# A graph layer on one core: VectorE's share of column copies 86.4 loads an octet in place of 85.33, and the end of the run in another order

## Chip, core and metric

The kernel runs on one core of one Trainium2 chip. The metric is the device time of one execution in microseconds, the median of several runs. Before the change it is 3294.95 us (three runs, 3292.81 to 3297.97).

## What is computed

A message passing step over 12500 nodes of 64 features and 400000 edges, sorted by destination, followed by a residual and a layer norm:

```python
m_in = jnp.concatenate([x[src], x[dst], edge_attr], axis=-1)    # 64 + 64 + 16
h = jax.nn.silu(m_in @ W1 + b1)
messages = jax.nn.silu(h @ W2 + b2)
agg = jax.ops.segment_sum(messages, dst, num_segments=12500)
node = jax.nn.silu(jnp.concatenate([x, agg], axis=-1) @ W3 + b3)
out = layernorm(x + node)
```

## The kernel before

The 400000 edges are 3125 tiles of 128, and eight tiles are an **octet** (391 of them; the last has five). The main loop (line 759) runs over octets. Since edges are sorted by destination, the targets of an octet lie within a window of 48 nodes, and sums of a window are made by a product with a one-hot matrix.

What an octet needs is the features of its edges' sources, tile by tile, and the kernel has three ways to get them, so that several engines share the work:

- **Gathers.** GpSimd issues one indirect DMA for each tile (`gather`, line 448), three octets ahead; five buffers `ga`.
- **Column copies.** Two tiles (a pair) can instead be filled column by column from node features that lie in SBUF (`columns`, lines 336 to 370), by ScalarE (line 367) or VectorE (line 369). The addresses are loaded into the engine's registers first, up to 16 (ScalarE) or 32 (VectorE) at a time; a column takes two of them, as the pair's two tiles lie on the two halves of the partitions. A full pair of 128 columns takes 256 loads.
- **Row copies.** SyncE fills a pair by 256 DMAs of one row (`rows`, line 397).

`shares` (line 314) tells how many loads each engine makes in an octet, in up to four parts of it. ScalarE makes 80 in four octets of five and 64 in the fifth. VectorE makes 96 in two octets of three and 64 in the third, as three or two chunks of 32. Lines 327 to 332 turn that into pairs: as soon as an engine has made 256 more loads, a pair of the octet after next is taken from the gathers. They go up to octet `len(octs) - QUIET - 2`, exclusive.

Through one turn `o` of the main loop, in the order that is written out by hand for TensorE, ScalarE, VectorE and SyncE: TensorE turns the one-hot matrix of octet o+1 (line 515) and computes its window's part (472); VectorE adds a finished window sum to `agg` (`add_window`, 592, six octets behind, three in the last eight), compares targets for o+2 (497), and makes its first chunk of columns; TensorE puts the sources in place and adds the edges' part (550, 553, 554) and ScalarE applies the first silu (557); VectorE copies window and one-hot matrix (477, 525) and makes its other chunks; TensorE makes window sums of an earlier octet (`add_up`, 581) and the second layer of another (566, 568), with ScalarE's second silu (572). The window sums lie in four slots of one PSUM tile, and TensorE's `add_up` waits for the last fold (592) ahead of it.

The nodes are finished in 25 groups of up to 512: `node_begin`, `node_x`, `node_sums` (619, 624, 630), `node_silu` (636), `node_add`, `node_stats`, then the root, the division (660) and `store` (664). All but the last two groups are spread over the main loop. The last two come at its end: the last but one in turn NO - 1 (lines 819 to 828; NO is 391), with the limits (701 to 718), which check that the windows held; the last behind the loop (881 to 893). The last group has 212 nodes, 53 partitions. `verdict` (720) sums the limits into `badi`, a flag; behind it all, every engine loads that flag into a register (line 106) and branches over a general version (line 108) that isn't run with these inputs.

Of the kernel before, what the change touches and what calls it, by code (L numbers as in the profile page):

```python
# [20 lines left out]
P = 128  # L21
G = 4
# [10 lines left out]
BEGIN = 6  # L33
TABLES = 7
ACOLS = (48, 32)
VCOLS = (32, 0, 32, 32)
ROWS = (256, 15)
LOADS = (16, 32)
XADDR = 16640
X2ADDR = XADDR + 50528  # L40
# [1 line left out]
HALF = 6144  # L42
OVER = 304
TURN = 195
QUIET = 5
DRAIN = 8
LAG = CT * P // 32
AHEADS = 256
# [6 lines left out]
@with_exitstack  # L55
def kernel(
    ctx: ExitStack,
    tc: tile.TileContext,
    x: bass.AP,
    xt: bass.AP,  # L60
    xt2: bass.AP,
    src_c: bass.AP,
    src_row: bass.AP,
    src_pair: bass.AP,
    dst_c: bass.AP,
    dst_row: bass.AP,
    attr_t: bass.AP,
    attr_2: bass.AP,
    base: bass.AP,
    w1: bass.AP,  # L70
    b1: bass.AP,
    w2: bass.AP,
    b2: bass.AP,
    w3: bass.AP,
    b3: bass.AP,
    out: bass.AP,
    edges: int,
):

    nc = tc.nc
    N, D = x.shape

    const = ctx.enter_context(tc.tile_pool(name="const", bufs=1))
    dram = ctx.enter_context(tc.tile_pool(name="dram", bufs=1, space=DRAM))
    pa = dram.tile([N, D], F32, name="pa")
    badi = const.tile([1, 1], I32, name="badi")
    ident = const.tile([P, P], F32, name="ident")
    make_identity(nc, ident)
    identb = const.tile([P, P], BF16, name="identb")  # L100
    nc.vector.tensor_copy(identb, ident)

    with ExitStack() as inner:
        windows(inner, tc, ident, identb, badi, pa, x, xt, xt2, src_c, src_row, src_pair, dst_c, dst_row, attr_t, attr_2, base, w1, b1, w2, b2, w3, b3, out, edges)

    flag = nc.values_load(badi[0:1, 0:1], min_val=0, max_val=4 * P,
                          skip_runtime_bounds_check_because="a count of partitions")
    with tc.If(flag > 0):
        general(tc, ident, x, xt, src_c, dst_c, dst_row, attr_t, w1, b1, w2, b2, w3, b3, out, edges)


def windows(ctx, tc, ident, identb, badi, pa, x, xt, xt2, src_c, src_row, src_pair, dst_c, dst_row, attr_t, attr_2, base, w1, b1, w2, b2, w3, b3, out, edges):
    nc = tc.nc
# [4 lines left out]
    NO = base.shape[1]  # L118
# [176 lines left out]
    with tc.tile_pool(name="gat", bufs=AHEAD + 2) as gat, \  # L295
# [18 lines left out]
        def shares(eng, o):  # L314
            if o < BEGIN:
                return (0, 0, 0, 0)
            if eng == ENG.Activation:
                return ACOLS if (o - BEGIN) % 5 < 4 else (ACOLS[0] - 16, ACOLS[1])
            return VCOLS if (o - BEGIN) % 3 < 2 else VCOLS[:3] + (0,)

        counts = {}
        for eng in (ENG.Activation, ENG.DVE):
# [274 lines left out]
        NG = len(groups)  # L597
        RB = 5
        v = nv.tile([P, 2 * RB, G, D], F32, name="v")
# [56 lines left out]
        def divide(q, i):  # L656
            p = groups[q][1] // G
            vi = v[:p, q % (2 * RB), i, :]
            j = q * G + i
            nc.vector.tensor_scalar(vi, vi, mv[:p, j, 0:1], rstd[:p, j:j + 1], op0=OP.subtract, op1=OP.mult)  # L660

        def store(q):
            c, n = groups[q]
            nc.sync.dma_start(out[c:c + n, :].rearrange("(p i) d -> p i d", i=G), v[:n // G, q % (2 * RB)])

# [11 lines left out]
        for q in range(rest):  # L679
            o = lead[due[q]] + LAST - 1  # L680
# [10 lines left out]
        for q0, q1 in batches:  # L691
            o = lead[due[q1 - 1]] + LAST + 2 * G
# [27 lines left out]
        def verdict(bad):  # L720
            pc = mis.tile([1, 4], F32, name="mm")
            nc.tensor.matmul(pc, onec, bad, start=True, stop=True)
            bs = nv.tile([1, 1], F32, name="bs")
            nc.vector.tensor_reduce(bs, pc, AX.X, OP.add)
            nc.vector.tensor_copy(badi, bs)
# [10 lines left out]
        folds = times({None: LAST, **{k: 3 for k in range(DRAIN)}})  # L736
# [17 lines left out]
        with tc.manual_schedule(engines={ENG.PE, ENG.Activation, ENG.DVE, ENG.SP}):  # L754
# [4 lines left out]
            for o in range(NO + 2):  # L759
# [3 lines left out]
                for k in range(0, NA, XC)[3 * o - 3:3 * o] if o else []:  # L763
                    n = min(XC, NA - k)
# [33 lines left out]
                for b in range(0, NO, 4):  # L798
                    if o == b + (4 if b < NO - DRAIN else 2):
                        bases(ENG.DVE, b)  # L800
                for q in folds.get(o, []):
                    add_window(q)
                if o == 1:
                    relative(0, CT, SCT)
                for k in range(3 * o - 3, 3 * o) if 1 <= o < 6 else []:
                    if k < 2 * len(parts):
                        c = parts[k // 2]
# [5 lines left out]
                def behind():  # L813
                    for q in adds.get(o, []):
                        add_up(q)
                    for q in seconds.get(o, []):
                        second_layer(q)

                if o == NO - 1:
                    assert NG == rest + 2 and groups[rest][0] + groups[rest][1] + LAG <= (NO - 4) // (CT // OT) * STEP  # L820
                    behind()
                    for i in range(G):
                        node_sums(rest, i)
                    node_silu(rest)
                    node_add(rest)
                    for i in range(G):
                        node_stats(rest, i)
                    bad = limits()
# [48 lines left out]
            for i in range(NO + 2, NO + LAST):  # L877
                for q in folds.get(i, []):
                    add_window(q)
            assert NO not in todo  # L880
            for i in range(G):
                node_sums(rest + 1, i)
            node_silu(rest + 1)
            node_add(rest + 1)
            for i in range(G):
                node_stats(rest + 1, i)
            verdict(bad)
            root(rest, NG)
            inverse(rest, NG)
            for q in range(rest, NG):  # L890
                for i in range(G):
                    divide(q, i)
                store(q)


@with_exitstack
# [255 lines left out]
```

## Time and profile before

| | before |
|---|---|
| median of three runs | 3294.95 us |
| the profiled execution | 3292.35 us |
| its span, first to last instruction | 3290.6 us |
| busy: ScalarE | 3109.2 us, 94% |
| busy: TensorE | 2486.1 us, 76% |
| busy: GpSimd | 2465.6 us, 75% |
| busy: VectorE | 2042.4 us, 62% |
| mean granted TensorE clock | 0.71 |
| column copies on ScalarE and VectorE | 14464 and 16000 |
| row copies | 6400 |

The profile comes from one execution. PE is TensorE, PEld its weight loads, DVE VectorE, ACT ScalarE, POOL GpSimd, SP SyncE; a q behind the name is its sequencer or its DMA queue. Loading registers, branches, semaphores and issuing DMAs don't count as busy. "issue" is idle time of an engine in which it waited for nothing that the profile shows; register loads fall into it. Window rows give the stretch, its length, the engine's busy time and its count of instructions, then the granted clock, the busy share of the DMA engines and GB/s.

### The profile page before, as it was taken

How to read it: one execution, taken by the hardware profiler on the slowest of the kernel's cores; microseconds unless marked ns; L12 is line 12 of the kernel's file. 1: busy time of each engine (PE TensorE's matmuls, PEld its weight loads, DVE VectorE, ACT ScalarE, POOL GpSimd, SP SyncE). 2: the span in 40 equal slices, each digit the busy share in tenths (PEclk: the TensorE clock that was granted, in tenths of full speed). 3: DMA queues.
4: the chain of work that ended last, by engine and by line, in shares of the span. 5: the costliest groups of instructions: out<-in, count | busy, mean ns of one | idle time of the engine just before them, and what ended most of it. 6: DMA issues, size and time to landing. Idle time of an engine off the chain costs nothing. (4 is left out here: it accounts for less than half of the span.)

```text
span 3290.6 us, 88339 instructions
## 1 busy us (share of the span) xinstructions
PE 2486.1 (76%) x15344; PEld 1705.0 (52%) x15344; DVE 2042.4 (62%) x18296; ACT 3109.2 (94%) x15306; POOL 2465.6 (75%) x2607
## 2 busy tenths in 40 slices
PE   7867777777777777767777777777877867777786
PEld 5545555555555545544454554545545545554554
DVE  5566666666666666666666666666666666666652
ACT  2799999999999999999999999999999999999991
POOL 7777777777777777777777777777777777777774
PEclk8787777777667677677767767766666676667666
DMA  7222222222222222221221222222222222222221
GB/s 148 50 41 40 43 41 40 43 41 40 45 44 44 42 42 40 41 43 38 48 46 39 43 41 40 43 43 43 45 41 42 40 44 41 43 44 45 39 42 33
DMA packets 160868, 147.82 MB, mean 45 GB/s; under 512 B 103748, under 2 KB 113718, under 8 KB 159526
## 3 DMA queue, kind: packets, MB, share of 16 engines
q0 software_dynamic: 83168, 85.33, 14.6%
q1 hardware_dynamic: 62624, 47.00, 5.7%
q10 hardware_dynamic: 14502, 9.75, 1.4%
q14 instruction: 447, 3.66, 0.4%
q8 instruction: 127, 2.08, 0.3%
HBM read 135.44 MB, written 6.40 MB: 43 GB/s over the span
## 5 line engine op out<-in xcount | busy, mean ns | idle before, releaser
L448 POOL DMA_INDIRECT ga<-pa,sc x2505 | 2375.6, 948 | 763.9 <-issue 666.0
L367 ACT ACTIVATE cx<-xs,x 128x1 f32 x14464 | 2789.5, 328 | 24.9 <-issue 19.5
L369 DVE TENSOR_TENSOR cx<-xs,x 128x4 uint8 x16000 | 1288.9, 154 | 1095.6 <-issue 1073.7
L581 PEld LDWEIGHTS pg<-eh,m 128*64 128x64 f32 x6250 | 296.8, 184 | 674.5 <-DVE agg L592 344.5
L550 PE MATMUL p<-ident,ga 128*128 128x128 f32 x1253 | 347.1, 364 | 393.7 <-DMA ga<-pa,sc 392.6
L568 PEld LDWEIGHTS p<-w2d,h 128*128 128x128 f32 x3126 | 536.7, 259 | 186.5 <-issue 186.5
L568 PE MATMUL p<-w2d,h 128*128 128x128 f32 x3126 | 632.5, 365 | 0.0
L554 PE MATMUL p<-oh,xw 128*128 128x512 f32 (+1 forms) x758 | 584.6, 866 | 0.0
L581 PE MATMUL pg<-eh,m 128*64 128x48 f32 x6250 | 352.8, 271 | 211.4 <-DVE agg L592 209.1
L550 PEld LDWEIGHTS p<-ident,ga 128*128 128x128 f32 x1253 | 220.4, 186 | 468.4 <-issue 433.2
L557 ACT ACTIVATE h<-p 128x512 f32<-128x512 f32 x391 | 243.1, 622 | 53.5 <-PE p L554 33.1
L515 PE MATMUL ph<-identb,eh 128*96 128x128 bf16 x1563 | 211.9, 276 | 99.9 <-DVE oh L525 96.4
L572 ACT ACTIVATE m<-p 128x512 f32<-128x512 f32 x391 | 242.6, 620 | 41.6 <-PE p L568 40.0
L525 DVE COPY oh<-ph 96x512 f32<-96x512 f32 x391 | 263.1, 673 | 1.9 <-PE ph L515 1.9
L515 PEld LDWEIGHTS <-eh 128*96 128x96 bf16 x1563 | 163.4, 163 | 136.5 <-DVE oh L525 122.4
L566 PE MATMUL p<-b2r,one 3*128 3x512 bf16 x391 | 193.3, 494 | 53.7 <-ACT m L572 53.2
L472 PE MATMUL mm<-w1bb,xr 65*96 65x128 f32 x782 | 221.5, 377 | 6.6 <-DMA xr<-in_xt 4.0
L497 DVE TENSOR_TENSOR eh<-wrow,dc 128x384 f32<-128x384 f32 x392 | 212.5, 542 | 11.3 <-PE wrow L624 6.9
L554 PEld LDWEIGHTS p<-oh,xw 128*128 128x128 f32 x758 | 175.8, 284 | 0.0
L472 PEld LDWEIGHTS mm<-w1bb,xr 65*96 65x96 f32 x782 | 139.9, 230 | 8.1 <-DMA xr<-in_xt 4.2
L553 PE MATMUL p<-cx,w1d 128*128 128x128 f32 x474 | 122.1, 368 | 0.0
L477 DVE TENSOR_TENSOR xw<-mm,mask 96x128 f32<-96x128 f32 x391 | 108.1, 276 | 20.6 <-PE mm L472 18.0
(106 smaller groups left out, 980.1 us busy)
## 6 DMA issues: line engine op xcount, KB each, us to landing
rx<-pa SPq DMA_DIRECT2D x6400, 0.2 KB
ga<-pa,sc POOLq DMA_INDIRECT x2505
oh<-in_attr SPq DMA_DIRECT2D x130, 192.0 KB
xr<-in_xt SPq DMA_DIRECT2D x391, 24.0 KB
cxi<-in_src_pair SPq DMA_DIRECT2D x238, 1.0 KB
xs<-in_xt ACTq DMA_DIRECT2D x6, 512.0 KB
pa<-v ACTq DMA_DIRECT2D x12, 256.0 KB
x<-in_xt ACTq DMA_DIRECT2D x6, 512.0 KB
```

The lines of the kernel that those rows point to most:

```text
L367: nc.scalar.activation(cols[key][:, k:k + 1], word(i, xb, XADDR), AF.Identity, bias=word(i + 4, x2b, X2ADDR))
L369: nc.vector.tensor_tensor(t[:, 4 * k:4 * k + 4], at(i, xb, XADDR), at(i + 4, x2b, X2ADDR), op=OP.max)
L448: nc.gpsimd.indirect_dma_start(out=ga[:, i, :], out_offset=None, in_=x if o < RAW else pa[:, :], in_offset=bass.IndirectOffsetOnAxis(ap=sc ...
L472: nc.tensor.matmul(pw[:E, :], winrow[o], w1bb.rearrange("k s m -> k (s m)"), start=True, stop=True)
L515: nc.tensor.matmul(ph[:E, i, :], eh[:, i, :, 1], identb, start=(i == 0), stop=(i == k - 1), skip_group_check=True)
L525: nc.vector.tensor_copy(oh[:E, :], ph[:E, :(n + 1) // 2].rearrange("p i e -> p (i e)"))
L550: nc.tensor.matmul(p1[:, i, :], g2.rearrange("p s d -> p (s d)"), ident, is_transpose=True, start=(i == c), stop=False, skip_group_check=True)
L554: nc.tensor.matmul(p1[:, :k], xw[o % 3], oh, start=False, stop=True, skip_group_check=True)
L557: nc.scalar.activation(h[:, :k], p1[:, :k], AF.Silu)
L568: nc.tensor.matmul(p2[:, 2 * i:2 * i + 2, :].rearrange("p s d -> p (s d)"), h[:, i, :], w2d, start=False, stop=(i == k - 1), skip_group_ch ...
L572: nc.scalar.activation(m[:, :n2], p2[:, :n2], AF.Silu)
L581: nc.tensor.matmul(pg[s * D:(s + 1) * D, :], m[:, i, :], eh[:, i // 2, :, s], start=(i < 2), stop=(i >= n - 2), skip_group_check=True)
```

## The change

VectorE's loads follow a rate of 27 chunks in 10 octets: an octet has three chunks or two, by the difference of a rounded line, 86.4 loads an octet. `QUIET` falls from 5 to 3. At the end, the fold that stood first in turn NO stands in turn NO - 1, behind that turn's sums and ahead of the node sums; the verdict stands ahead of the last group's sums; every engine loads the flag ahead of the last store; and `store` splits a group whose partitions are no multiple of 16, here 53 into 48 and 5.

```diff
+VRATE = (27, 10)
...
-QUIET = 5
+QUIET = 3
...
-        windows(inner, ...)
-
-    flag = nc.values_load(badi[0:1, 0:1], min_val=0, max_val=4 * P,
-                          skip_runtime_bounds_check_because="a count of partitions")
+        flag = windows(inner, ...)
+
     with tc.If(flag > 0):
...
-            return VCOLS if (o - BEGIN) % 3 < 2 else VCOLS[:3] + (0,)
+            n = (o + 1 - BEGIN) * VRATE[0] // VRATE[1] - (o - BEGIN) * VRATE[0] // VRATE[1]
+            return VCOLS if n == 3 else VCOLS[:3] + (0,)
...
         def store(q):
             c, n = groups[q]
-            nc.sync.dma_start(out[c:c + n, :].rearrange("(p i) d -> p i d", i=G), v[:n // G, q % (2 * RB)])
+            to, p = out[c:c + n, :].rearrange("(p i) d -> p i d", i=G), n // G
+            for a, b in ((0, p // 16 * 16), (p // 16 * 16, p)):
+                if b > a:
+                    nc.sync.dma_start(to[a:b], v[a:b, q % (2 * RB)])
...
-                for q in folds.get(o, []):
+                for q in folds.get(o, []) if o != NO else []:
                     add_window(q)
...
                 if o == NO - 1:
...
                     behind()
+                    for q in folds[NO]:
+                        add_window(q)
                     for i in range(G):
                         node_sums(rest, i)
...
             assert NO not in todo
+            verdict(bad)
             for i in range(G):
                 node_sums(rest + 1, i)
...
                 node_stats(rest + 1, i)
-            verdict(bad)
             root(rest, NG)
             inverse(rest, NG)
             for q in range(rest, NG):
                 for i in range(G):
                     divide(q, i)
+                if q == NG - 1:
+                    flag = nc.values_load(badi[0:1, 0:1], min_val=0, max_val=4 * P,
+                                          skip_runtime_bounds_check_because="a count of partitions")
                 store(q)
+    return flag
```

More of the change, by code (lines that the diff above doesn't have):

```diff
@@ L103 @@
     with ExitStack() as inner:
-        windows(inner, tc, ident, identb, badi, pa, x, xt, xt2, src_c, src_row, src_pair, dst_c, dst_row, attr_t, attr_2, base, w1, b1, w2, b2, w3, b3, out, edges)
-    flag = nc.values_load(badi[0:1, 0:1], min_val=0, max_val=4 * P,
-                          skip_runtime_bounds_check_because="a count of partitions")
+        flag = windows(inner, tc, ident, identb, badi, pa, x, xt, xt2, src_c, src_row, src_pair, dst_c, dst_row, attr_t, attr_2, base, w1, b1, w2, b2, w3, b3, out, edges)
     with tc.If(flag > 0):
```

## The prediction

> **What bounds the kernel now.** I read the groups by line first, then the same work by stretches, then the waits of each stretch, and last the order of time at the end. Per group the columns are line, engine, operation, count, then busy us and mean ns, then the idle time before them.
>
> ```profile
> L448 POOL DMA_INDIRECT ga<-pa,sc x2505 | 2375.6, 948 | 763.9 <-issue 666.0 <-DMA ga<-pa,sc 69.2 <-PE p L550 8.8
> L448 POOL DMA_INDIRECT ga<-in_x,sc x94 | 89.1, 948 | 30.7 <-issue 25.3 <-DMA ga<-in_x,sc 1.9 <-PE mm L472 1.6
> L369 DVE TENSOR_TENSOR cx<-xs,x 128x4 uint8 x16000 | 1288.9, 154 | 1095.6 <-issue 1073.7 <-ACT m L572 9.1 <-ACT cx L367 4.9
> ```
>
> GpSimd issues 2505 + 94 = 2599 gathers. Busy and idle together are 3259.3 us, and that idle time is issue gaps: GpSimd gathers from the first microseconds until 30 us before the end, without a real wait. VectorE makes 16000 column copies, 125 tiles of 128; 1000 loads of 32 registers stand before groups of 16 copies.
>
> Two stretches follow, each cut exactly at starts of line 525 (one per octet): first the gathers alone, then line 525 alone.
>
> ```profile
> 354.99:1088.47 733.48, 555.09 (x586) 0.72 0.21 43
> 1334.27:3070.66 1736.39, 1313.99 (x1386) 0.70 0.21 43
> ...
> 354.99:1088.47 733.48, 60.59 (x90) 0.72 0.21 43
> 1334.27:3070.66 1736.39, 141.33 (x210) 0.70 0.21 43
> ```
>
> A gather costs 1736.39 / 1386 = **1.253 us**. In the late stretch an octet takes 1736.39 / 210 = **8.268 us**, which is 6.6 gathers: GpSimd's pace. In the early one it takes 733.48 / 90 = **8.150 us**: there VectorE runs faster than the gathers, because the engines lag behind them from the start-up and are making it good, 90 x 0.118 = 10.6 us in this stretch. What limits them there is in the waits: TensorE's two largest kinds in question early, VectorE's own early, TensorE's late, and TensorE's in the last 70 us (from 3193 to 3264).
>
> ```profile
> PE pg L581 <- DVE agg L592: 130.3, 56, 4.8
> PE p L550 <- DMA ga<-pa,sc: 13.4, 11, 2.5
> ...
> DVE cx L369 <- ACT m L572: 3.4, 3, 1.4
> DVE cx L369 <- ACT cx L367: 2.3, 2, 1.2
> ...
> PE p L550 <- DMA ga<-pa,sc: 318.7, 218, 3.1
> ...
> PE p L550 <- DMA ga<-pa,sc: 13.2, 9, 3.2
> ```
>
> Early, TensorE waits for VectorE (130.3 us) and hardly for gathers; VectorE waits 5.7 us for others. So 8.150 us is about VectorE's own pace at full load. Late, TensorE waits 318.7 us for gathers. Hence the kernel is bound by GpSimd with only 1.4% of room on VectorE, plus a tail of 30 us behind the last gather.
>
> **The change part by part.**
>
> *Columns.* By the code, VectorE's tiles are counted as loads(o) >= 256k, with o up to 383 and 85.33 x 377 = 32170: 125. With 86.4 it is 86.4 x 379 = 32745 at o = 385: **127**. With the old limit, 86.4 x 377 = 32572, it is also 127, and ScalarE has 76.8 x 377 = 28954 or 76.8 x 379 = 29107, 113 both times. So the limit of three octets adds no tile by itself. Two tiles more are four gathers fewer, 2595: 4 x 1.253 = **5.0 us**, while GpSimd stays the bound. (Half of it falls before octet 180, half in the last tile.)
>
> The price is on VectorE: 16 more loads of 32 with 16 copies each, 0.0333 per octet. One load's period, from two starts that follow with other work hidden between:
>
> ```profile
> 563.09 1.31 DVE L369 TENSOR_TENSOR cx<-xs,x 128x4 uint8 x16 [1.54 <-issue]
> ...
> 565.88 1.30 DVE L369 TENSOR_TENSOR cx<-xs,x 128x4 uint8 x16 [0.69 <-issue]
> ```
>
> That is 2.79 us. The nearest lower bound is the group's total, (1288.9 + 1095.6) / 1000 = 2.38 us. For an upper one I take the 8.150 us of an octet over its 2.667 loads, 3.06 us. So an octet gets 0.079 to 0.102 us longer on VectorE; I take 0.093, the measured period: 8.150 + 0.093 = **8.243 us**. GpSimd's new pace is 6.592 x 1.253 = 8.260. VectorE still fits, by 0.017 us instead of 0.118. The lag of the start-up is then not made good in the first thousand us but over the whole run: about 345 octets x 0.017 = 6 us of the 10.6. Some 5 us stand when the columns end. Behind them come eight octets without columns, where TensorE now waits 13.2 us for gathers; a late TensorE finds those gathers there and uses up that time first. I leave **1 us** of loss; 0 is possible, and at VectorE's upper price (8.252) 8 us would enter the last stretch, with at most some 5 left over. ScalarE's columns are unchanged, and it kept up with 8.150 us in the early stretch. The new tiles end two octets later, under gathers that still run.
>
> One rule speaks against this. The Trainium skill, "SBUF — State Buffer", section "SBUF: two separate sides", has VectorE and GpSimd share a port pair that a VectorE operation with two SBUF inputs holds whole against a GpSimd operation that reads SBUF. It is weighed as a rival below.
>
> *The fold before the node sums.* The end of the run, TensorE and then VectorE in order of time:
>
> ```profile
> 3260.05 0.67 PE L581 MATMUL pg<-eh,m 128*64 128x48 f32 x16 [0.75 <-ACT m L572]
> 3261.97 1.97 PE L630 MATMUL wrow<-w3s,agg 128*128 128x64 f32 x8
> 3264.11 0.81 PE L554 MATMUL p<-oh,xw 128*128 128x384 f32 x2
> 3269.00 1.10 PE L581 MATMUL pg<-eh,m 128*64 128x48 f32 x16 [4.07 <-DVE agg L592]
> 3270.45 1.65 PE L568 MATMUL p<-w2d,h 128*128 128x128 f32 x6
> 3272.74 0.87 PE L581 MATMUL pg<-eh,m 128*64 128x48 f32 x10 [0.64 <-ACT m L572]
> 3273.91 1.11 PE L630 MATMUL mm<-w3s,agg 128*53 128x64 f32 x8 [0.30 <-DVE agg L592]
> 3274.94 0.19 PE L722 MATMUL mm<-bad,onec 128*1 128x4 f32 x2
> ...
> 3268.59 0.14 DVE L717 TENSOR_SCALAR bad<-lim 128x1 f32<-128x1 f32 x1
> 3268.65 0.19 DVE L592 TENSOR_TENSOR agg<-agg,pg 128x48 f32 x1
> 3270.13 0.20 DVE L592 TENSOR_TENSOR agg<-agg,pg 128x48 f32 x1 [1.28 <-PE pg L581]
> 3273.65 0.20 DVE L592 TENSOR_TENSOR agg<-agg,pg 128x48 f32 x1 [3.31 <-PE pg L581]
> 3277.37 0.14 DVE L725 CAST badi<-bs 1x1 int32<-1x1 f32 x1
> 3277.90 1.87 DVE L660 TENSOR_SCALAR v<-v,mv,rstd 128x64 f32<-128x64 f32 x8
> ```
>
> The sums of the last octet but one are ready for TensorE at 3264.92, but start at 3269.00, because the fold that frees them stands on VectorE behind the node group's statistics and the limits, until 3268.65. The change puts that fold ahead: its input ends at 3260.72, so it is done by 3261.0, a microsecond before line 630 at 3261.97, which now also waits for it. Then TensorE runs on from 3264.92; at the old spacing of 3.74 us (3269.00 to 3272.74) the last sums could start at 3268.7. What is late next is the following fold, still behind the limits: at 3268.65, and TensorE answers a fold's start 0.35 us later, 3269.0. So the last sums start at 3269.0 instead of 3272.74, and all that hangs on them moves by **3.7 us**: last fold 3269.9, line 630 at 3270.2, last division done at 3276.0 instead of 3279.8.
>
> *Verdict, flag and store.* These rows give when each sequencer loads the flag, branches and closes (duration min/median/max in ns, then first to last start):
>
> ```profile
> L106 POOLq TENSOR_LOAD <-badi x1: 511/511/511, 3277.5 to 3277.5; - x1
> L106 SPq TENSOR_LOAD <-badi x1: 627/627/627, 3280.1 to 3280.1; - x1
> L108 POOLq COMPARE_BRANCH  x1: 53/53/53, 3278.1 to 3278.1; - x1
> L108 SPq COMPARE_BRANCH  x1: 54/54/54, 3280.8 to 3280.8; - x1
> L108 POOLq EVENT_SEMAPHORE  x5: 17/43/43, 3281.3 to 3284.2; - x5
> L1148 POOLq DRAIN  x3: 40/107/4230, 3285.5 to 3290.3; - x3
> ...
> L664 SPq DMA_DIRECT2D out<-v x25: 250/371/377, 897.9 to 3279.8; - x25
> ...
> SPq L108 <- SPq L108: 2.8, 1, 2.8
> ```
>
> The end is GpSimd's: its drain of 4.23 us begins at 3285.5 and ends at 3289.7, 0.9 us before the span's 3290.6; the span ends 13.1 us behind the flag's write, 3277.5. It was written that late because it stands behind the second group's statistics. The verdict now stands right behind the last fold (3269.9, done 3270.1); line 722 fits into TensorE's wait for that fold, and two short VectorE operations write the flag at about 3270.4 while VectorE would wait for the node sums anyway. So the flag is **7.1 us** earlier, and with it GpSimd's closing: 3270.4 + 13.1 = 3283.5. SyncE comes before that: store of the first group at 3275.2, flag load 0.63 us behind it, then the two parts of the last store, 0.25 us each, and the branch at 3276.8 (3280.8 - 4.0); 2.8 us of its own gap and some 2 us of semaphores end at 3282. The second part of the store therefore costs nothing beside GpSimd's drain; uncovered it would cost 0.3 us. From GpSimd's view all 7.1 us count. The other bound: if something in GpSimd's 3278.1 to 3284.2 waits for SyncE, only 4.0 us. I take the first, since no wait for SyncE shows in GpSimd's list there.
>
> A rule bears on that choice: the Trainium skill, "Runtime: NRT & Kernel Launch", section "Instruction fetch mechanics", says that a taken branch to a far target waits for a fetch of instructions. By it GpSimd's gap hangs on its own branch, and the tail gives 7.1 us, not 4.0.
>
> *Sum.* -5.0 - 7.1 + 1.0 = **-11.1 us** against the profiled span. That execution took 3292.35 us, 1.75 over its span and 2.6 below the median 3294.95; I take the difference from the median: 3283.9, **3284 us** (-0.34%).
>
> **The rivals.**
> - *The lag stays* (chance 0.20). VectorE's price is at or above its upper bound, all 10.6 us reach the last octets, and a good part is not regained there, since TensorE may meet other waits. For it: the margin of 0.017 us is a fifth of the price itself. Against: 13.2 us of waiting there. Loss 5 to 11 instead of 1: around **3291**.
> - *GpSimd's closing hangs on SyncE* (0.12): -5.0 - 4.0 + 1 = -8: **3287**.
> - *VectorE becomes the bound, slower* (0.13). Extra loads fall into octets that had two; the fold and the turned copy come later, and TensorE, which already waits 130 us for VectorE in 90 octets, passes that on. It ends slower by 6.6 us when the loss is 19: (19 + 13.2 - 10.6) / 375 = 0.058 us per octet over GpSimd's 8.260, a price of 5 us per load, 1.8 times the measured one. At twice the price: 8.336, 375 x 0.076 + 10.6 - 13.2 = 26 us of loss, **3309**. Against it: VectorE's period of 2.79 us holds with other work between.
> - *The copies hold up the gathers* (0.03). 256 copies more at 1288.9 / 16000 = 0.081 us each would take 20.6 us from GpSimd in the worst case: 3284 + 20.6 = **3305**. Against it is this row from 3200 on, where VectorE copies almost nothing:
>
> ```profile
> L448 POOL DMA_INDIRECT ga<-pa,sc x49 | 46.2, 944 | 14.9 <-issue 13.1 <-DMA ga<-pa,sc 0.9 <-PE p L550 0.3
> ```
>
>  (46.2 + 14.9) / 49 = 1.247 us without copies against 1.253 with 6.5 copies to a gather: 0.9 ns a copy, 0.2 us for 256. (It is the case that the SBUF page's rule would give; this trace does not bear it out.)
> - *It doesn't do what it says* (0.02): no tile or fold moves; 3295.
>
> **How the numbers follow.** The forecast has 0.50, its own range 3281 to 3288. Range for all: **3280** (no loss, 1 us; line 568 in the tail as quick as at 3260, some 0.8 us; and the 2.1 us by which the lowest run of before lies under its median) to **3300** (the lag kept, 3294, and VectorE 0.016 us an octet over GpSimd's pace, 375 x 0.016 = 6); outside it stand the slower cases. A change of 0.2%, 6.6 us, is about what a measurement of this kernel can tell from none: faster is below 3288.4, slower above 3301.5. Faster: 0.47 of the forecast, 0.10 of the SyncE case, 0.03 of the lag: 0.60. Slower: 0.13 and 0.02 of the copies: 0.15. Same: 0.25.
>
> **What would show it.** Right: 2595 gathers at 1.253 us; line 525 in the early stretch at 8.23 to 8.26 us an octet; TensorE's wait for gathers, 318.7 us, falls to a fraction, while its wait for line 592 grows; line 592 stands ahead of line 630 near the last gather plus 0.2 us, and the 4.07 us wait is gone; the flag is written some 9.6 us behind the last gather's end (16.7 before), and the drain follows 8 us later. Wrong: GpSimd gathers end where they did, an octet of VectorE costs over 8.26 us, or TensorE is still behind at the last gather.

## The result, and the profile after

| | before | after |
|---|---|---|
| median (six runs each) | 3294.66 us | 3280.49 us |
| lowest and highest | 3292.81 to 3297.97 | 3279.66 to 3285.47 |
| ratio, 95% interval | | 0.9958 [0.9947, 0.997] |
| the profiled execution | 3292.35 us | 3281.77 us |
| its span | 3290.6 us | 3280.0 us |
| end of the last gather | 3260.81 us | 3256.85 us |

The medians differ by 14.2 us, the two profiled executions by 10.6; the forecast's sum was 11.1. The profiled execution of before was 2.3 us better than its median, that of after 1.3 us worse than its own: 10.6 + 2.3 + 1.3 = 14.2. All that is read from these two traces stands against the 10.6. Two single executions, 5237.74 us among the eleven of e3 below and 6457.25 us among those of the kernel before beside e4 to e7, lie far from the rest of theirs and stand in no ratio. In the kernel after, the store is line 667, the flag's load 899, the branch 107, the verdict's product 725, the flag's write 728, and the closing 1157; the other lines that matter here keep their numbers.

The groups of GpSimd's gathers and VectorE's copies, after:

```profile
L448 POOL DMA_INDIRECT ga<-pa,sc x2501 | 2372.4, 949 | 762.7 <-issue 649.9 <-DMA ga<-pa,sc 89.3 <-PE p L550 7.0
L448 POOL DMA_INDIRECT ga<-in_x,sc x94 | 89.2, 949 | 31.0 <-issue 26.2 <-PE p L545 2.0 <-DMA sc<-in_src_c 1.2
```

There are 2595 gathers, four fewer, and (2372.4 + 762.7) / 2501 = 1.254 us each, as before (1.253). GpSimd still hardly waits for anybody.

Line 525 alone in the two stretches of the prediction, after:

```profile
354.99:1088.47 733.48, 59.89 (x89) 0.71 0.18 43
1334.27:3070.66 1736.39, 141.97 (x211) 0.70 0.18 43
```

Starts, not counts, give the pace here, since one octet in 89 is 0.09 us: by the starts of line 525 an octet takes 8.235 us early (octets 38 to 128) and 8.234 late (158 to 368), where it was 8.150 and 8.268. VectorE is at its own pace in both stretches now. TensorE's waits in the early stretch, the late one, and from 3193 to 3264, after:

```profile
PE pg L581 <- DVE agg L592: 130.2, 62, 4.2
PE p L550 <- DMA ga<-pa,sc: 7.8, 6, 2.3
...
PE pg L581 <- DVE agg L592: 260.2, 131, 4.6
PE ph L515 <- DVE oh L525: 86.4, 100, 2.2
PE p L550 <- DMA ga<-pa,sc: 72.3, 50, 2.9
...
PE p L550 <- DMA ga<-pa,sc: 13.2, 8, 3.2
```

The late wait for gathers fell from 318.7 us to 72.3, and TensorE waits 260.2 us for the folds instead. Yet in the last 70 us it again waits 13.2 us for gathers: it has caught up with GpSimd before the end.

The end, TensorE and then VectorE in order of time, after:

```profile
3252.20 0.45 PE L550 MATMUL p<-ident,ga 128*128 128x128 f32 x1 [2.19 <-DMA ga<-pa,sc]
3252.43 1.91 PE L554 MATMUL p<-oh,xw 128*128 128x512 f32 x2
...
3259.44 1.98 PE L630 MATMUL wrow<-w3s,agg 128*128 128x64 f32 x8
3261.25 0.50 PE L550 MATMUL p<-ident,ga 128*128 128x128 f32 x3
3261.59 0.81 PE L554 MATMUL p<-oh,xw 128*128 128x384 f32 x2
3262.33 0.67 PE L581 MATMUL pg<-eh,m 128*64 128x48 f32 x16
...
3266.47 0.84 PE L581 MATMUL pg<-eh,m 128*64 128x48 f32 x10 [2.34 <-DVE agg L592]
3267.24 0.19 PE L725 MATMUL mm<-bad,onec 128*1 128x4 f32 x2
3267.61 1.11 PE L630 MATMUL mm<-w3s,agg 128*53 128x64 f32 x8 [0.17 <-DVE agg L592]
```

```profile
3258.24 0.20 DVE L592 TENSOR_TENSOR agg<-agg,pg 128x48 f32 x1 [2.62 <-PE pg L581]
...
3266.13 0.19 DVE L592 TENSOR_TENSOR agg<-agg,pg 128x48 f32 x1
3267.35 0.20 DVE L592 TENSOR_TENSOR agg<-agg,pg 128x48 f32 x1 [1.03 <-PE pg L581]
...
3267.66 0.14 DVE L728 CAST badi<-bs 1x1 int32<-1x1 f32 x1
...
3271.61 1.87 DVE L660 TENSOR_SCALAR v<-v,mv,rstd 128x64 f32<-128x64 f32 x8
```

The fold at 3258.24 stands ahead of line 630, and the sums at 3262.33 start with no wait (4.07 us before). What is late next is, as forecast, the fold behind the limits, 3266.13: the last sums wait 2.34 us for it. The flag is written at 3267.8, ahead of the last group's statistics and 5.7 us ahead of the last division's end, 3273.48.

The closing of the two sequencers, after:

```profile
L899 POOLq TENSOR_LOAD <-badi x1: 514/514/514, 3267.8 to 3267.8; - x1
L899 SPq TENSOR_LOAD <-badi x1: 479/479/479, 3273.0 to 3273.0; - x1
L107 POOLq COMPARE_BRANCH  x1: 53/53/53, 3268.4 to 3268.4; - x1
L107 SPq COMPARE_BRANCH  x1: 54/54/54, 3274.9 to 3274.9; - x1
L107 POOLq EVENT_SEMAPHORE  x5: 17/43/43, 3271.1 to 3271.4; - x5
L1157 POOLq DRAIN  x3: 40/107/4045, 3273.3 to 3279.7; - x3
L1157 SPq DRAIN  x3: 7/7/12, 3279.1 to 3279.4; - x3
L667 SPq DMA_DIRECT2D out<-v x26: 331/375/874, 894.3 to 3274.0; - x26
```

GpSimd's long drain begins at 3273.3, before SyncE has even branched (3274.9), and ends at 3277.3. SyncE now ends last. One issue of line 667 took 0.874 us where the median is 0.375: it is the store's second part of five rows, since SyncE's branch follows the issue at 3274.0 by 0.9 us.

So the 10.6 us of the two traces split in four: the gathers end 3.96 sooner (3260.81 to 3256.85). TensorE starts the last octet's line 550 (3261.25) 4.40 us behind the last gather, where it was 2.96: 1.43 lost. The last sums start 5.22 us behind that line, where it was 8.96: 3.74 won. From the last division's end to the span's end it takes 6.5 us, where it was 10.8: 4.3 won. -3.96 + 1.43 - 3.74 - 4.3 = -10.6. Each of the first two terms depends on the pair of traces: e0, below, has the kernel before end its gathers 2.6 us later.

### The profile page after: what moved, and what is told of

Read it like the earlier page. It is cut to its first block, busy times and chain, and to the rows that moved or that the text cites. A ratio compares the mean times of both kernels' runs of the same rounds, so it can differ in the third digit from the quotient of the medians.

```text
span 3280.0 us, 88619 instructions
## 1 busy us (share of the span) xinstructions
PE 2460.8 (75%) x15346; PEld 1722.2 (53%) x15346; DVE 2063.0 (63%) x18554; ACT 3106.6 (95%) x15306; POOL 2462.5 (75%) x2603
## 5 line engine op out<-in xcount | busy, mean ns | idle before, releaser
L448 POOL DMA_INDIRECT ga<-pa,sc x2501 | 2372.4, 949 | 762.7 <-issue 649.9
L369 DVE TENSOR_TENSOR cx<-xs,x 128x4 uint8 x16256 | 1309.3, 154 | 1095.2 <-issue 1075.1
L581 PEld LDWEIGHTS pg<-eh,m 128*64 128x64 f32 x6250 | 281.9, 175 | 928.0 <-DVE agg L592 758.6
L581 PE MATMUL pg<-eh,m 128*64 128x48 f32 x6250 | 336.4, 262 | 467.1 <-DVE agg L592 465.1
L568 PE MATMUL p<-w2d,h 128*128 128x128 f32 x3126 | 641.1, 369 | 0.0
L568 PEld LDWEIGHTS p<-w2d,h 128*128 128x128 f32 x3126 | 543.5, 262 | 159.0 <-issue 159.0
L554 PE MATMUL p<-oh,xw 128*128 128x512 f32 (+1 forms) x758 | 575.2, 853 | 0.0
L550 PE MATMUL p<-ident,ga 128*128 128x128 f32 x1251 | 313.6, 370 | 118.6 <-DMA ga<-pa,sc 117.9
L515 PE MATMUL ph<-identb,eh 128*96 128x128 bf16 x1563 | 221.6, 285 | 158.0 <-DVE oh L525 154.2
L550 PEld LDWEIGHTS p<-ident,ga 128*128 128x128 f32 x1251 | 229.3, 197 | 144.0 <-issue 126.0
L472 PE MATMUL mm<-w1bb,xr 65*96 65x128 f32 x782 | 230.0, 390 | 6.2 <-DMA xr<-in_xt 3.8
```

Of the source, the lines that this page charges most:

```text
L369: nc.vector.tensor_tensor(t[:, 4 * k:4 * k + 4], at(i, xb, XADDR), at(i + 4, x2b, X2ADDR), op=OP.max)
L448: nc.gpsimd.indirect_dma_start(out=ga[:, i, :], out_offset=None, in_=x if o < RAW else pa[:, :], in_offset=bass.IndirectOffsetOnAxis(ap=sc ...
L472: nc.tensor.matmul(pw[:E, :], winrow[o], w1bb.rearrange("k s m -> k (s m)"), start=True, stop=True)
L515: nc.tensor.matmul(ph[:E, i, :], eh[:, i, :, 1], identb, start=(i == 0), stop=(i == k - 1), skip_group_check=True)
L550: nc.tensor.matmul(p1[:, i, :], g2.rearrange("p s d -> p (s d)"), ident, is_transpose=True, start=(i == c), stop=False, skip_group_check=True)
L554: nc.tensor.matmul(p1[:, :k], xw[o % 3], oh, start=False, stop=True, skip_group_check=True)
```

## The experiments

Three things were open behind this result: whether columns and end give what each is said to give, and add up; whether GpSimd's closing hangs on the flag (my theory) or on SyncE (the rival); and how near VectorE is to being the bound (the rival on the slower side). Each kernel was compared with the kernel before on the same chip. One table serves for the ends. Line 550 (of the last octet) and the span's end are in us behind the last gather's end, "between" is the difference of the two, and all come from each kernel's trace:

| kernel | gathers | line 550 | span's end | between | GpSimd, branch to drain |
|---|---|---|---|---|---|
| before | 2599 | 2.96 | 29.75 | 26.8 | 7.4 |
| e0, before again | 2599 | 6.28 | 33.42 | 27.1 | 7.7 |
| e3, fold only | 2599 | 7.27 | 30.84 | 23.6 | 7.3 |
| e4, flag only | 2599 | 3.05 | 25.77 | 22.7 | 6.7 |
| e2, end only | 2599 | 7.27 | 26.59 | 19.3 | 6.5 |
| e1, columns only | 2595 | 3.01 | 28.04 | 25.0 | 5.8 |
| after | 2595 | 4.40 | 23.13 | 18.7 | 4.9 |
| e6, store whole | 2595 | 3.21 | 21.20 | 18.0 | 5.1 |
| e7, store on two queues | 2595 | 6.46 | 23.91 | 17.5 | 4.8 |

**e0: before, unchanged.**

> The kernel before, unchanged, with a second profile. Ratio 1.000. It tells what two profiles of one kernel differ by: I expect the last gather's end within 1.5 us of 3260.8 (its pitch of 1.2537 us has gaps that come and go) and the 29.8 us behind it within 1 us.

Measured: 3296.45 us, ratio 0.9998 [0.9989, 1.0007]. Its trace has a longer span, 3296.8 us, than the first profile's 3290.6. The gathers end 2.6 us later, and the tail is 3.7 us longer: within 1.5 and within 1 were expected, so both missed. The stretch from 3260 to 3265, all engines (busy and count of each, then the clock, the DMA share, GB/s), before and e0:

```profile
3260.00:3265.00 5.00, 4.87 (x38) 3.97 (x38) 0.57 (x2) 1.02 (x3) 0.81 (x1) 1.00 0.07 13
```

```profile
3260.00:3265.00 5.00, 4.25 (x36) 3.32 (x37) 0.20 (x1) 1.19 (x2) 2.79 (x3) 0.50 0.14 26
```

The granted clock was 1.00 in one execution of the same program and 0.50 in the other, and line 550 of the last octet starts 2.96 us behind the last gather in one and 6.28 in the other. The same holds for the others: in the 5 us on either side of the last gather's end the clock is 1.00 in before, e1, e4 and e6, which start it at 3.0 to 3.2 us, and 0.50 to 0.59 in e2, e3 and e7, which start it at 6.5 to 7.3, whatever their columns or order; after has 0.66 ahead of it and 1.00 behind, and 4.4 us. I take the clock for the cause, since TensorE's own work takes longer there too: lines 554 and 581 of one octet take 1.02 and 0.67 us at the fast clock, up to 1.91 and 1.10 at the slow one. So the column "between" is what tells the edits apart, and a difference of 3 us in one profile's tail tells nothing.

**e1: the columns alone** (the end as before).

> The rate of 27 chunks in ten octets and the limit of three octets, with the end of the run as before. My theory (the gathers pace the kernel, VectorE still fits under them): 2595 gathers, 4 to 5 us faster than before in the time, line 525 at 8.23 to 8.26 us an octet from 355 to 1088 us, TensorE's wait for gathers between 1334 and 3070 us down from 319 us to under 100, and the stretch from the last gather's end to the span's end 30 us as before, at most 2 longer. Rival, the lag stays: that stretch is 5 to 11 us longer and the time is within 3 us of before or above it. Rival, VectorE becomes the bound: slower by 6 us or more.

```diff
+VRATE = (27, 10)
...
-QUIET = 5
+QUIET = 3
...
-            return VCOLS if (o - BEGIN) % 3 < 2 else VCOLS[:3] + (0,)
+            n = (o + 1 - BEGIN) * VRATE[0] // VRATE[1] - (o - BEGIN) * VRATE[0] // VRATE[1]
+            return VCOLS if n == 3 else VCOLS[:3] + (0,)
```

Measured: 3288.36 us, 0.9981 [0.9972, 0.999]: 8.2 us less by the medians (3296.57 before, on that chip), 6.3 by the ratio and 3 to 9 by its interval, where 4 to 5 were expected. The gathers' own part is there, 2595 of them. Where the last one ends varies from trace to trace, but the two counts keep apart: 3260.81, 3263.39, 3263.70, 3261.66 and 3266.16 us with 2599 gathers (before, e0, e2, e3, e4), 3256.85, 3257.76, 3257.78 and 3258.35 with 2595 (after, e1, e6, e7). The means are 5.5 us apart. An octet takes 8.236 us early and 8.249 late. One expectation missed: TensorE's late wait for gathers should have fallen below 100 us. e1, in the late stretch (its line 552 is 550 of before):

```profile
PE p L552 <- DMA ga<-pa,sc: 223.9, 149, 3.1
```

The lag behind the gathers with which an execution leaves its start-up isn't the same each time: counted from 2.5 us behind the start of the octet's last gather, the first silu of octet 8 came 21.9 us later in the trace of before, 19.1 in that of after and 16.7 in that of e1; at octet 130 it was 8.5 in after and 3.9 in e1, which had made it good. Why the start-up differs is open. The table shows one more thing: "between" is 25.0 for e1, where the end was not touched. GpSimd's way from its branch to its drain is 5.8 us instead of 7.4; it is shorter in each kernel with 2595 gathers. Of GpSimd's two gaps there, 3278.1 to 3281.3 and then up to 3284.2 before, the second is gone after (3271.1 to 3271.4 for all five semaphores) and in e1. So the columns alone, with GpSimd ending last, gave about 1.6 us at the closing that no step had. What the second gap waited for no row names. The table's last column holds a second difference: with 2599 gathers GpSimd's way takes 7.3 to 7.7 us where the flag comes late (before, e0, e3) and 6.5 to 6.7 where it comes early (e2, e4); with 2595 it is 5.8 late and 4.8 to 5.1 early.

**e2: the end alone** (old rate of columns).

> The new end of the run with the old rate of VectorE, 2599 gathers. My theory: the stretch from the last gather to the span's end falls from 29.8 us to 22 to 23.5 us, and the time by 6 to 8 us; pace of the octets as before, with TensorE's wait for gathers near 319 us between 1334 and 3070 us. Rival, all of the gain is the columns': under 3 us faster. If this and the columns alone add up to the whole change's 14 us, nothing is lost between them; if this one alone gives 11 us or more, the columns gave little.

```diff
+            to, p = out[c:c + n, :].rearrange("(p i) d -> p i d", i=G), n // G
+            for a, b in ((0, p // 16 * 16), (p // 16 * 16, p)):
...
-                for q in folds.get(o, []):
+                for q in folds.get(o, []) if o != NO else []:
...
+                    for q in folds[NO]:
+                        add_window(q)
...
+            verdict(bad)
             for i in range(G):
                 node_sums(rest + 1, i)
...
+                    flag = nc.values_load(badi[0:1, 0:1], min_val=0, max_val=4 * P,
```

Measured: 3288.43 us, 0.9976 [0.9966, 0.9986]: 8.1 us less by the medians, 7.9 by the ratio and 5 to 11 by its interval (the prediction's 7.1 for this part lies inside). The tail of 26.59 us is longer than expected, since this trace has the clock of 0.50 at line 550, 7.27 us; "between" fell by 7.5 us against before. 0.9981 and 0.9976 make 0.9957, where the whole change has 0.9958: within their intervals, some 3 us to either side, the two parts add up, and no loss between them is seen.

**e3: the fold alone.**

> Only the fold of turn NO moved ahead of the node sums; verdict, flag and store as before. My theory: the 4.07 us wait at line 581 goes, the last sums start 5.2 us after the last octet's line 550 instead of 9.0, the flag's write and the last division are 3.7 us earlier against the last gather, the span ends 26 us after the last gather, and the time is 3.7 us less. Rival, that the fold is answered by the limits all the same and nothing moves: 0 us.

```diff
-                for q in folds.get(o, []):
+                for q in folds.get(o, []) if o != NO else []:
...
+                    for q in folds[NO]:
+                        add_window(q)
```

Measured: 3293.47 us, 0.9988 [0.9978, 0.9997], 1 to 7 us less by the interval, and "between" 3.2 us less than before, 3.5 less than e0. The tail itself, 30.84 us where 26 was expected, has the slow start of line 550 in it (7.27 us). e3's TensorE at the end:

```profile
3268.93 0.84 PE L550 MATMUL p<-ident,ga 128*128 128x128 f32 x3
3269.57 1.48 PE L554 MATMUL p<-oh,xw 128*128 128x384 f32 x2
3270.99 1.09 PE L581 MATMUL pg<-eh,m 128*64 128x48 f32 x16
...
3274.73 0.87 PE L581 MATMUL pg<-eh,m 128*64 128x48 f32 x10 [0.64 <-ACT m L572]
```

The wait of 4.07 us is gone and the last sums come 5.8 us behind line 550. The clock is slow here, so TensorE itself takes 3.74 us between the two sums and the fold behind the limits is no longer what they wait for. In the trace of after, with the fast clock, they do wait for it (2.34 us). So the step gains about the same in both traces, 3.2 and 3.74 us, though the last sums wait for different things.

**e4: verdict and flag alone** (the store in one piece).

> Only the verdict ahead of the last group's sums and the flag's load ahead of the last store; fold and store as before. My theory (GpSimd's closing hangs on the flag alone): GpSimd's branch follows the last fold by about 1 us, its drain is over before SyncE's, the span ends about 6.5 us after the last division instead of 10.8, and the time is 3.5 to 4.5 us less than before. Rival, GpSimd's closing hangs on SyncE: the drain still ends last, and the time is at most 0.5 us less.

```diff
             assert NO not in todo
+            verdict(bad)
...
-            verdict(bad)
...
+                if q == NG - 1:
+                    flag = nc.values_load(badi[0:1, 0:1], min_val=0, max_val=4 * P,
```

Measured: 3291.47 us, 0.9982 [0.9973, 0.9991], 5.8 us less by the medians (3297.27 before, on that chip) where 3.5 to 4.5 were expected; the interval holds 3 to 9. "Between" fell by 4.1 us. e4's closing:

```profile
L106 POOLq COMPARE_BRANCH  x1: 53/53/53, 3280.1 to 3280.1; - x1
L106 SPq COMPARE_BRANCH  x1: 54/54/54, 3285.7 to 3285.7; - x1
...
L1150 POOLq DRAIN  x3: 40/107/4230, 3286.8 to 3291.7; - x3
L1150 SPq DRAIN  x3: 7/7/13, 3290.6 to 3291.3; - x3
```

One expectation missed: GpSimd still ends last; its long drain ends at 3291.1, while SyncE comes to its own first drain at 3290.6. But where GpSimd's drain begins settles the closing. Before, GpSimd's drain began 7.4 us behind its own branch and 4.7 behind SyncE's. Here it begins 6.7 behind its own and 1.2 behind SyncE's, and in the trace of after 1.6 us ahead of SyncE's. It hangs on the flag and on GpSimd's own gaps, and the rival that has it hang on SyncE falls. A rule of the Trainium skill fits the rows: "Runtime: NRT & Kernel Launch", section "Instruction fetch mechanics", says that a taken branch to a target outside the loaded instructions waits until that target is fetched. It gives no time for that; here GpSimd's first gap behind the branch is 2.7 us (after) and SyncE's 2.8.

**e5: 88 loads an octet**, three in octets of four, otherwise as after.

> The changed kernel with 11 chunks in four octets, 88 loads an octet, 130 tiles on VectorE and 2589 gathers. By the price of 2.79 us a chunk VectorE's octet would be 8.150 + 0.0833 x 2.79 = 8.38 us (8.36 by what the change itself showed, 2.55), against 8.25 for the gathers: VectorE becomes the bound, about 0.12 us x 375 = 45 us behind the gathers at the end of the columns, of which the last octets take back some 13. Gathers end 7.5 us earlier, so 20 to 30 us slower than the changed kernel. If it is faster or the same, VectorE's room was larger than I think. If copies hold up the gathers, their median pitch of 1.249 us grows.

```diff
-VRATE = (27, 10)
+VRATE = (11, 4)
```

Measured: 3325.82 us, 1.0089 [1.0073, 1.0104]: 2589 gathers, and 29 us slower than before, 45 slower than after by the medians (40 between the two profiled spans), where 20 to 30 slower than after was expected. The octet's pace was as expected, 8.366 us early and 8.377 late. TensorE's waits in the late stretch of e5, GpSimd's over the run, and its group of gathers:

```profile
PE pg L581 <- DVE agg L592: 320.4, 165, 5.1
PE ph L515 <- DVE oh L525: 114.0, 122, 2.0
```

```profile
POOL ga L448 <- PE p L550: 40.8, 37, 3.7
```

```profile
L448 POOL DMA_INDIRECT ga<-pa,sc x2495 | 2367.5, 949 | 790.8 <-issue 658.9 <-DMA ga<-pa,sc 74.0 <-PE p L550 40.8
```

TensorE waits for no gather any more, and GpSimd waits 40.8 us for TensorE to give buffers back: VectorE is the bound. The expected size forgot that the start-up's lag isn't made good either when VectorE has no room, which is about 10 us of what was missed; the rest is open. The lag of the first silu behind the gathers grows from 17 to 35 us and stays there, since GpSimd can be no more than its buffers ahead. In the last octets, where there are no columns, it falls from 32.4 to 19.3: 13.1 us taken back, about the 13.2 of waiting that the prediction had read there.

This run answers the rival of the copies that hold up gathers too. Without the waits for TensorE a gather took (2367.5 + 790.8 - 40.8) / 2495 = 1.249 us, with the most copies of all kernels here; by the same reckoning it was (2375.6 + 763.9 - 8.8) / 2505 = 1.250 before, and the median from start to start is 1.249 in both. The rule that would give that rival (the Trainium skill, "SBUF — State Buffer", section "SBUF: two separate sides") isn't borne out for indirect gathers in these rows.

**e6: the last store in one piece**, otherwise as after.

> The changed kernel with the last store in one piece of 53 partitions. SyncE now ends last, and the second part costs it 0.9 us: if only its issuing counts, the branch comes 0.9 us sooner after the last division and the span ends 0.9 us sooner. If the landing of 53 rows one after another counts (3.9 us from issue in the kernel before), SyncE waits for it at its third semaphore and the end is the same within 0.3 us or later. In the time nothing can be told: within 1 us.

```diff
-            for a, b in ((0, p // 16 * 16), (p // 16 * 16, p)):
-                if b > a:
-                    nc.sync.dma_start(to[a:b], v[a:b, q % (2 * RB)])
+            nc.sync.dma_start(out[c:c + n, :].rearrange("(p i) d -> p i d", i=G), v[:n // G, q % (2 * RB)])
```

Measured: 3280.77 us, 0.995 [0.9936, 0.9964]. By the time it can't be told from after. e6's SyncE:

```profile
L107 SPq COMPARE_BRANCH  x1: 54/54/54, 3273.4 to 3273.4; - x1
L107 SPq EVENT_SEMAPHORE  x8: 17/17/17, 3276.2 to 3277.3; - x8
...
L664 SPq DMA_DIRECT2D out<-v x25: 280/375/381, 898.2 to 3273.0; - x25
```

No issue takes over 0.381 us, and SyncE branches 0.46 us behind the last division (3272.91) instead of 1.43. From the last division to the span's end it is 6.07 us against 6.51. So half of what the branch gained is lost again: SyncE's eight semaphores behind the branch take 1.1 us (3276.2 to 3277.3) where they took 0.6 in after (3277.7 to 3278.3). One of them is the whole store's own, and it comes about 4.0 us behind the store's issue. Both cases of the expectation are in play, and splitting the store cost 0.44 us net. Its issue isn't the same each time, either: the parts of 48 and 5 rows took 0.331 and 0.874 us in after, 0.620 and 0.627 in e2, 0.639 and 0.352 in e5, in all 0.99 to 1.25, where one of 53 rows takes 0.25 to 0.28.

**e7: the five rows issued from ScalarE**, otherwise as after.

> The changed kernel with the store's second part, five rows, issued from ScalarE instead of SyncE. SyncE's branch should come 0.9 us sooner after the last division and the span end 0.9 us sooner, ScalarE's own closing staying ahead of SyncE's; if ScalarE's branch (2.5 us, then its semaphores) comes last instead, nothing is gained. In the time 1 us, hardly to be told.

```diff
-                    nc.sync.dma_start(to[a:b], v[a:b, q % (2 * RB)])
+                    (nc.scalar if a else nc.sync).dma_start(to[a:b], v[a:b, q % (2 * RB)])
```

Measured: 3282.38 us, 0.9952 [0.9939, 0.9966]; from the last division to the end 5.53 us, 1.0 less than after. The time doesn't show it: line 550 came at 6.46 us in this trace. None of e6, e7 and after can be called the best.

**e8, e9, e10: another chip.** e8 is the kernel before without 26 of its gathers (those tiles keep an earlier octet's rows, so the sums of their edges are left wrong). e9 and e10 are e7 with a pair's 256 row copies spread over 14 and 13 octets instead of 15.

> The kernel before with 26 gathers left out, the eighth tile's in every fourteenth octet from 26 on; those tiles hold an earlier octet's rows, so that part of the sums is not the reference's. VectorE and ScalarE do what they did. If the gathers alone pace the kernel, 26 x 1.254 = 32.6 us less, at most 2 us given back, since an octet's gathers take 8.19 us and VectorE's octet 8.15. If another engine paced it, the time would fall by less than half of that.

> The changed kernel with the store's second part on ScalarE's queue, and SyncE's row copies at 256 in 14 octets instead of 15: 26 tiles of rows, 2593 gathers. The gathers end 2.5 us earlier, VectorE's octet 8.235 us still fits under 8.26; with the shorter closing 2.5 to 3.5 us less than the changed kernel. If SyncE's queue delays the window loads, slower than it.

> The same at 256 rows in 13 octets: 28 tiles of rows, 2589 gathers, 7.5 us fewer for GpSimd, whose octet comes to 8.25 us against VectorE's 8.235, so that the start-up's lag stays until the last octets, which take back 13 us of it. 4 to 8 us less than the changed kernel; if VectorE's octet is the bound, as in the run with 88 loads, no gain or up to 5 us slower. SyncE issues 19.7 rows an octet at 0.34 us, 6.8 us with 1.5 for its other DMAs: if that is too much, the octet grows to SyncE's and the time by 10 us or more.

The edit of e8, then that of e9 (13 in e10):

```diff
+                if i // 2 < len(slots[o]) + (o in rpairs) or (i == 7 and o >= 26 and o % 14 == 12):
+                    continue
```

```diff
-ROWS = (256, 15)
+ROWS = (256, 14)
```

Measured: 0.9904 [0.9889, 0.9919], 1.0263 [1.0249, 1.0277] and 1.069 [1.0675, 1.0705], but against a median of 4963.35 us for the kernel before on that chip. e8's longest wait of TensorE:

```profile
PE mm L472 <- DMA xr<-in_xt: 1254.5, 217, 12.1
```

There TensorE waited 1254.5 us for transfers of SyncE's queue, in which the row copies stand, and more row copies made it slower still. e8 was 45.5 us faster where 32.6 were expected, and e9 and e10 came out as the case that each named for a SyncE too slow. These three say nothing of the change; e9 and e10 were not run on a chip of the usual time.

**e11: e8 once more**, on a chip where the kernel before takes 3298.25 us.

> The kernel before with 26 gathers left out, once more, since on the first chip the kernel before itself took 4963 us and was not paced by its gathers. If the gathers alone pace the kernel, 26 x 1.254 = 32.6 us less than before, at most 2 us given back, since an octet's gathers then take 8.19 us and VectorE's octet 8.15. If another engine paced it, less than half of that.

Measured: 3278.09 us (3270.4 to 3282.58), 0.9935 [0.9922, 0.9949]: 20.2 us less, where 26 gathers at 1.253 us make 32.6 and at most 2 were to be given back. A miss. In the profiled execution, the slowest of the five (3282.58 us), the gathers did end 26.5 us sooner (3234.27), but the last octet's line 550 came 23.6 us behind. e11, TensorE's waits in the late stretch, and from 3060 to 3265:

```profile
PE pg L581 <- DVE agg L592: 258.0, 121, 3.9
PE ph L515 <- DVE oh L525: 81.3, 92, 2.2
PE p L550 <- DMA rx<-pa: 29.0, 7, 5.5
...
PE mm L472 <- DMA xr<-in_xt: 24.1, 12, 3.9
...
PE p L550 <- DMA rx<-pa: 10.0, 2, 5.3
```

Line 550 waits for no gather in the late stretch. With the old rate of columns an octet took 8.153 us early but 8.194 late, where the starts of an octet's gathers are 8.198 apart, so the lag was never made good; it was large from the start, 34.7 us at octet 8 against 21.9 in before. Behind VectorE stand SyncE's transfers (24.1 and 10.0 us). GpSimd bounds the kernel, but with little below it: in this run 20.2 of 32.6 us came through, and less of that by the gathers, since in its trace the closing, too, is 4.3 us shorter than before (6.4 us from the last division to the span's end, 10.8 before). How the loss splits between the start-up, VectorE and SyncE stays open.

## Why the prediction was right, point by point

- *GpSimd's gathers bound the kernel, VectorE is close behind.* Right: 2595 gathers at the same pitch, and 88 loads an octet already turn it over (e5). But what lies behind the gathers isn't VectorE alone: with 26 gathers fewer an octet took 8.194 us late, not 8.150 (e11), and TensorE waited there for SyncE's transfers as well as for VectorE.
- *Columns, -5.0.* Right: 3.96 between these two traces, 5.5 between the means of all nine (e1). The 1.0 that the pair lacks is no more than traces differ by, and no wait shows behind it: start to start, the median of all gathers is 1.249 us in each kernel; the rest are longer ones here and there, 55 of them over 1.3 us in the trace of before, 62 after, 83 in e1, 82 in e0. The mean was 1.2537 before and 1.2541 after, 2595 times 0.0004.
- *VectorE's price, 2.79 us a chunk.* Mis-sized a little, inside its bounds: (8.235 - 8.150) / 0.0333 = 2.55 us, and from e5 (8.366 - 8.150) / 0.0833 = 2.59. The period between two starts probably holds some of the other work that would have been done anyway. So the room left was 0.030 us an octet instead of 0.017 (the starts of an octet's gathers are 8.264 apart late).
- *The lag, 1 us of loss.* The size came out (1.43), the reason did not: that is luck. TensorE had caught up: it waited 2.19 us for the last gather of the last octet but one. The start behind that wait is 4.7 us ahead of the last gather's end in both traces (3252.20 and 3256.14). What follows is longer, by the clock: lines 554 and 581 took 1.91 and 1.10 us in after, and before's TensorE has

```profile
3256.14 0.30 PE L550 MATMUL p<-ident,ga 128*128 128x128 f32 x1 [1.12 <-DMA ga<-pa,sc]
3256.28 1.02 PE L554 MATMUL p<-oh,xw 128*128 128x512 f32 x2
3257.23 0.67 PE L581 MATMUL pg<-eh,m 128*64 128x48 f32 x16
```

  Those are 0.89 and 0.43 us of the 1.43, and e0 loses more at this place without any change. No cost of VectorE's lag shows in this trace.
- *The fold, -3.7.* Right: -3.74 in the trace, and -3.2 alone (e3). The next late fold was the one named, in the trace of after; in e3, at the slow clock, none was late.
- *Verdict and flag, -7.1 with the fold.* Right in mechanism (e4), and the part as a whole: e2 has -7.5 in "between" and -7.9 by the ratio. The flag came 10.95 us behind the last gather instead of 9.6, of which 1.4 is the clock of the point above.
- *"The second part of the store costs nothing beside GpSimd's drain."* This step failed. The part took 0.874 us to issue, not 0.25, and GpSimd was done at 3277.3, since its second gap went away. So SyncE ends last, and the split is uncovered: 0.44 us (e6), near the 0.3 named for that case, though only because the whole store's landing takes back half of what it saves.
- *The sum.* 11.1 forecast, 10.6 between the profiles. Part of that closeness is luck: the columns gave 1.0 less in this pair and the start of line 550 lost 0.4 more, while the closing gave 4.3 where the sum had 3.4 (7.1 less the fold's 3.7). The medians moved 14.2: of the 3.6 us between, 2.3 lie on before's side, whose profiled execution was a favourable one, and 1.3 on after's. The fast clock at before's end may be part of that; no run shows how much. GpSimd's second gap was in no step; that it went only made room, since SyncE ends last in after, and e2, which has the gap, comes to the same 6.5 us from the last division to the end.
- *The rivals.* The lag that stays, GpSimd hanging on SyncE, and copies that hold up gathers: not borne out (after, e4, e5). VectorE as the bound is real, one step further on: 1.6 loads more an octet cost some 40 to 45 us (e5 against after).

## What to carry to other kernels

Where two engines run within a per cent of each other, read the second one's pace in a stretch in which it catches up with the first, add the price of each piece of work to it, and stop before the sum passes the first one's pace: here 0.085 us more an octet still fitted and won some 5 us, and 0.216 was too much and made the kernel 29 us slower than before, the better end included. Behind the last producer look for what stands in a queue only by the order of writing (a fold behind statistics, a flag behind a store), since each microsecond there counts whole. And take a second profile of the unchanged kernel before reading a few microseconds at an end.

## What the runs showed of the hardware that was not expected

- The granted TensorE clock behind the last gather is 1.00 in some executions of one program and 0.50 in others, and with it the start of line 550 moves by 3 us (2.96 and 6.28 us, before and e0).
- A store in parts of 48 and 5 rows took SyncE 0.99 to 1.25 us to issue (after, e2, e5), a whole one of 53 rows 0.25 to 0.28; the whole one's semaphore came about 4.0 us behind its issue (e6).
- GpSimd's gap behind its last branch came in two pieces, 7.4 us from branch to drain, in the kernel before, and in one piece, 4.9 us, after the change; the second piece is there in each kernel with 2599 gathers and in none with fewer, and no row names the cause.
- On one chip the same program took 4963 us; TensorE waited 1254.5 us for transfers of SyncE's queue there (e8).
